# Row blocks turned by VectorE and exchanged by way of memory in place of TensorE transposes, for the middle sequences

## The chip, the cores and the metric

One core of one Trainium2 chip runs the whole program. The metric is the device time of one execution in microseconds, as the median of several runs. All data are 32-bit floats, apart from a few small 16-bit tables of the router.

## What is computed

The reference is one transformer layer on 8 sequences of 512 tokens with 256 features: causal attention with 16 heads of 128 (four heads share one key and value group), and a feed-forward part with a router that sends each token to 6 of 64 experts, beside one shared expert. Both parts normalize the rows ahead of their products and normalize what they add.

```python
x = x + _layernorm(attn(_layernorm(x), wq, bq, wkv, bkv, wo))
x = x + _layernorm(ffn(_layernorm(x), gate_w, w_gate, w_up, w_down, sh_gate, sh_up, sh_down))
# attn: q, k, v = x@wq + bq, x@wkv + bkv; q, k += sinusoids; softmax(causal(q k^T / sqrt(128))) v; @ wo
# ffn: top 6 of softmax(x@gate_w.T), each expert silu(x@w_gate) * (x@w_up) @ w_down, plus the shared expert
```

The kernel's matmuls take their operands with the dimension that is summed over on the partitions. A normalized block of rows has tokens on the partitions, so it must be turned, features onto partitions, before the projections (tile `xnt`, first half of the layer) and before the shared expert and the router (tile `xt2`, second half).

## The kernel before

A sequence is held as four tiles of 128 tokens. The main loop runs over 128 heads, k = 16 b + s for sequence b and head s. The order on each engine is written out by hand; every engine takes its instructions in that order. One round of the loop holds, in this order on TensorE:

- the scores of head k (`psc`, L289): four matmuls of 128, 256, 384 and 512 columns, for the causal shape. VectorE subtracts the mask and finds the least value (`e`, L293), ScalarE takes the exponential (L296). The scores go to the pool `ps_s` of three PSUM banks.
- the output projection of head k-3 (`po`, L361), the queries of head k+1 (`pq`, L276; VectorE adds bias and sinusoids to make `qt`, L279), and the weighting of the values of head k-2 (`pav`, L349).

Between these stand, on the other engines, `weigh(k)` on GpSimd (L306: `e` times the reciprocal of its sum) and `turned(k-1)`. The latter turns the weights of the head before: VectorE transposes blocks of 32 x 32 (`eb`, L322), SP writes the four groups of 32 partitions to memory (`ex_d`, L327), and SP reads the whole back (`et`, L330), so that blocks land on the partitions on which they belong. SP's queue waits for the four writes to land before it issues the read. `et` is wanted by `pav` one round later.

Beside the heads of a sequence b run two slower strands, tied to a head number and a place in the round (A, B, M, D, from the weigh to the end of the round):

- `prepare(b+1)`, the first half for the next sequence: load the rows of `x`, statistics (`scales`), normalize (`normal`, tile `xn`), `turn`, four `keys`, four `values`. Its steps are taken from an iterator `ahead`, so many in each round. For most sequences the rows are loaded at the end of head 6, normalized in head 8 ahead of the queries, and turned at the end of head 8.
- `feed_forward(b-1)`, the second half of the sequence before: `copies` 2D, `residual_sums` 4A, `store` 5B (SP writes `x1`, L774), `rows` 6A (tile `xg`), `turn` 6M, `shared_gate` 7A (`psg`, `psu`, L708, which read `xt2`), the router (`gate` at 8A, and the steps "r" after it), the other products of the shared expert (the steps "f").

Both call `transpose_rows`, in which TensorE turns 128 x 128 blocks into a PSUM bank of `ps_s`, and ScalarE copies one bank (L109), VectorE the other (L112) back. The tiles named here share tags with others: one buffer under "xn" holds `o`, then `xn`; one under "y" holds the router's logits `lg`, later `y`.

From head 94 on the experts' products run beside the heads (`routed`); sequences from EARLY = 5 on have a second half with more steps. These parts, and the end of the program, are as they were in the changed kernel.

Of the kernel before, what the change touches and what calls it, by code (L numbers as in the profile page):

```python
# [11 lines left out]
F32 = mybir.dt.float32  # L12
# [7 lines left out]
P = 128  # L20
B, T, E = 8, 512, 256
NT = B * T
NI = T // P
BS = 32
AT = [0, 4, 7, 9]
NB = AT[-1] + 1
NC = E // P
# [12 lines left out]
EARLY = 5  # L40
# [4 lines left out]
def sandwich_kernel(ctx, tc, x, wq, bq_t, wkv, bk_t, bv, wo, gate_wt, w_gate, w_up, w_down,  # L45
                    sh_gate_t, sh_up_t, sh_down_t, pe_t, out):
    nc = tc.nc
# [11 lines left out]


    ex_d = [dram.tile([P, NI, NB * BS], F32, tag=f"ex{n}_d", name=f"ex{n}_d") for n in range(2)]
    x1_d = dram.tile([NT, E], F32, tag="x1_d", name="x1_d")
    xg_d = dram.tile([ET_ROWS + 1, ROW], F32, tag="xg_d", name="xg_d")
    y_d = dram.tile([2 * (ET_ROWS + CAP), E], F32, tag="y_d", name="y_d")
# [49 lines left out]
    def transpose_rows(dst, rows, name):  # L114

        for c in range(NC):
            pt = ps_s.tile([P, T], F32, tag="s", name=f"pt_{name}_{c}")
            for i in range(NI):
                nc.tensor.transpose(pt[:, ts(i, P)], rows[:, i, ts(c, P)], ident)
            (on_act, on_dve)[c](dst[:, c, :], pt)  # L120


    with ExitStack() as part:
# [4 lines left out]
        p1 = pool("p1", 1)  # L128
# [96 lines left out]
        def prepare(b):  # L225

            s = seqs[b] = {"kt": []}

            def rows():
                s["x"] = load_x(b) if b else x_first  # L230

            def scales():
                s["scales"] = norm_scales(tiles_of(s["x"]), f"a{b}")

            def normal():
                mv, rs = s.pop("scales")
                s["xn"] = p1.tile([P, NI, E], F32, tag="xn", name=f"xn_{b}")
                for i in range(NI):
                    normalize(s["xn"][:, i, :], s["x"][:, i, :], mv, rs, i)

            def turn():
                s["xnt"] = p2.tile([P, NC, T], F32, tag="xnt", name=f"xnt_{b}")
                transpose_rows(s["xnt"], s["xn"], f"a{b}")

            def keys(g):
                pk = ps_m.tile([P, T], F32, tag="m", name=f"pk_{b}_{g}")
                for c in range(NC):
                    nc.tensor.matmul(pk, lhsT=wkv_sb[:, c, g, 0, :], rhs=s["xnt"][:, c, :],  # L248
                                     start=c == 0, stop=c == NC - 1)
# [12 lines left out]

            yield rows
            yield scales
            yield normal
            yield turn
            for g in range(G):
# [44 lines left out]
        def turned(k):  # L312
            l = live[k]
            eb = p2.tile([P, NI, NB, BS], F32, tag="eb", name=f"eb_{k}", bufs=1)
            for i in range(NI):
                for js in ([0, 1], [2, 3]):
                    js = [j for j in js if j <= i]
                    if not js:
                        continue
                    at, step = AT[js[0]] + i - js[0], AT[js[-1]] - AT[js[0]] - 1  # L320
                    blocks = eb[:, :, at : at + step * (len(js) - 1) + 1 : max(step, 1), :]
                    nc.vector.transpose(  # L322
                        blocks.rearrange("p c j t -> p j c t"),
                        l["e"][i][:, js[0] * P : (js[-1] + 1) * P].rearrange("p (j c t) -> p j c t", c=NI, t=BS))
            ex = ex_d[k % 2]
            for a in range(NI):
                nc.sync.dma_start(out=ex[:, a, :].rearrange("(c s) f -> s c f", s=BS),  # L327
                                  in_=eb[ts(a, BS)].rearrange("s c n t -> s c (n t)"))
            l["et"] = p2.tile([P, NI, NB, BS], F32, tag="et", name=f"et_{k}")
            nc.sync.dma_start(out=l["et"].rearrange("s a n t -> s (a n t)"), in_=ex.rearrange("p a f -> p (a f)"))  # L330

# [346 lines left out]
        def shared(b, xt2, l, banks="mmmmmm"):  # L678
# [22 lines left out]
            for n, (f0, fw) in reversed(list(enumerate(SH_CHUNKS))):  # L701
                mw = min(P, fw + NX // 2)
                pgu = []
                for w_sb, name in ((sg_sb, "psg"), (su_sb, "psu")):
                    tag = next(banks)
                    pp = {"m": ps_m, "s": ps_s}[tag].tile([P, T], F32, tag=tag, name=f"{name}_{b}_{n}")
                    for c in range(NC):
                        nc.tensor.matmul(pp[:mw, :], lhsT=w_sb[:, c, ds(f0, mw)], rhs=xt2[:, c, :],  # L708
                                         start=c == 0, stop=c == NC - 1)
                    pgu.append(pp)  # L710
                if fw < P:
# [40 lines left out]
        def feed_forward(b):  # L752
# [3 lines left out]
            l = {}  # L756
# [37 lines left out]
            def go(which, n=1):  # L794
                return lambda: [next(l[which]) for _ in range(n)]
# [7 lines left out]
            if b < B - 2:  # L803
                steps |= {"9A": go("f"), "9B": go("f"), "11A": go("f"), "11B": go("f")}
            if b < EARLY:
                return steps | {"10A": go("r"), "10D": go("r", 2),
                                "11D": go("r", 2), "12A": go("f"), "12D": go("r", 2), "13A": go("f"), "13D": go("r", 2)}
# [135 lines left out]
        def side(s, place):  # L943
            behind.pop(f"{s}{place}", lambda: None)()
            if not b:
                for u in rest.get(f"{s}{place}", ()):
                    u()

        for k in range(NK):
# [28 lines left out]
            if active and not finishing:  # L978
# [19 lines left out]
            for _ in range((0, 0, 0, 0, 0, 0, 1, 0, 1, 1, 2, 1, 1, 1, 2, 1)[s] if b == EARLY + 1 else  # L998
                           (0, 0, 0, 0, 0, 0, 1, 1, 1, 1, 1, 1, 1, 1, 2, 1)[s]):
                next(ahead, lambda: None)()  # L1000
# [97 lines left out]
```

## Time and profile before

| | |
|---|---|
| median of 3 runs | 1431.23 us (1428.58 to 1433.54) |
| profiled execution | 1433.63 us |
| its span, first to last instruction | 1431.9 us |
| mean granted TensorE clock | 0.995 |
| busy: TensorE, VectorE, ScalarE, GpSimd | 97%, 62%, 35%, 30% |
| DMA | 252.03 MB, mean 176 GB/s |
| HBM read, written | 143.01 MB, 107.74 MB |

The profile gives, for one execution, the busy time of each engine, the chain of work that ended last, groups of equal instructions with their mean duration and what ended the idle time before them, and on request windows and timelines. PE is TensorE, PEld its weight load, DVE VectorE, ACT ScalarE, POOL GpSimd, and SPq the queue of SP. L119 is line 119 of the kernel before. A 32-bit matmul is two instructions in the trace, a transpose one. Matmuls overlap, so a mean duration (0.593 us for a query's 512 columns) is longer than the distance from one to the next.

### The profile page before, as it was taken

The page shows a single profiled execution, that of the slowest core. Times are in us where ns is not written, and L with a number is a line of the kernel's source. Part 1 is how long each engine was busy: PE and PEld are TensorE (multiplying, and loading weights), DVE is VectorE, ACT ScalarE, POOL GpSimd, SP SyncE. Part 2 cuts the span into 40 slices and gives each one's busy share as a digit, 9 for nine tenths or more (in the row PEclk, how much of TensorE's full clock was granted, in tenths as well). Part 3 has the DMA queues.
Part 4 walks back from the last instruction along what each step waited for, and adds up shares of the span by engine and source line. Part 5 has one row for each costly group of instructions (what it writes and reads, how often), then busy time and mean ns, then how long its engine had stood idle before and what let it go on. Part 6 is the DMA issues. An engine that isn't in the chain of part 4 may idle for free.

```text
span 1431.9 us, 18567 instructions
## 1 busy us (share of the span) xinstructions
PE 1393.9 (97%) x5310; PEld 850.3 (59%) x5310; DVE 888.9 (62%) x3097; ACT 505.3 (35%) x1442; POOL 428.9 (30%) x686
## 2 busy tenths in 40 slices
PE   9999999999999999999999999999999999999895
PEld 5666665666656665656556665655556555556563
DVE  5565576656765576656765577566666545577634
ACT  2333333234422343234422343233443333444421
POOL 2231242113311232123211232124544344444311
PEclk9999999999999999999999999999999999999998
DMA  7765565356554564356544564358998789778702
GB/s 239 206 199 142 146 174 162 110 132 171 168 144 124 147 185 136 99 156 168 161 127 128 162 195 129 99 155 275 308 286 250 227 232 264 201 235 265 234 15 82
DMA packets 160791, 252.03 MB, mean 176 GB/s; under 512 B 16412, under 2 KB 136189, under 8 KB 160685
## 3 DMA queue, kind: packets, MB, share of 16 engines
q1 hardware_dynamic: 125869, 201.52, 48.4%
q10 hardware_dynamic: 28672, 39.85, 9.0%
q0 software_dynamic: 6144, 9.44, 3.3%
q8 instruction: 43, 0.70, 0.2%
q14 instruction: 63, 0.52, 0.1%
HBM read 143.01 MB, written 107.74 MB: 175 GB/s over the span
## 4 chain that ended last, share of the span: by engine, by line
PE 83%; DVE 8%; DMA 2%; ACT 2%; issue 2%; POOL 1%; SPq 0%; DVEq 0%; ACTq 0%; POOLq 0%
PE pav L349 17%; PE psc L289 16%; PE po L361 13%; PE pq L276 13%; PE pk L248 4%; PE pv L259 4%; PE psg L708 3%; PE psu L708 3%; PE pgu L549 2%; PE py L735 2%; DVE eb L322 2%; PE pd L575 2%; ACT e L296 2%; DMA ex_d<-eb 1%; PE pth L566 1%
## 5 line engine op out<-in xcount | busy, mean ns | idle before, releaser
L306 POOL TENSOR_SCALAR e<-e,recip 128x128 f32<-128x128 f32 x508 | 269.7, 571 | 775.3 <-DVE recip L303 762.4
L296 ACT ACTIVATE e<-e,least 128x128 f32<-128x128 f32 (+3 forms) x512 | 285.7, 559 | 350.4 <-DVE least L293 332.6
L289 PE MATMUL psc<-kt,qt 128*128 128x128 f32 (+3 forms) x1024 | 307.7, 438 | 9.9 <-DVE least L293 3.5
L349 PE MATMUL pav<-et,v 128*128 128x512 f32 (+3 forms) x1024 | 297.1, 433 | 1.4 <-DMA et<-ex_d 1.1
L349 PEld LDWEIGHTS pav<-et,v 128*128 128x128 f32 x1024 | 193.6, 190 | 161.0 <-issue 113.8
L293 DVE CUSTOM_DVE_ANT_0 e<-psc,mask 128x128 f32<-128x128 f32 (+3 forms) x512 | 232.2, 479 | 58.1 <-PE psc L289 52.2
L361 PE MATMUL po<-wo_sb,ao 128*128 128x256 f32 x1024 | 245.0, 383 | 0.7 <-ACT ao L109 0.7
L276 PE MATMUL pq<-xnt,wq_sb 128*128 128x512 f32 x512 | 240.9, 593 | 0.3 <-ACT sc L388 0.3
L361 PEld LDWEIGHTS po<-wo_sb,ao 128*128 128x128 f32 x1024 | 194.2, 191 | 72.5 <-issue 40.3
L109 ACT COPY ao<-pav 128x512 f32<-128x512 f32 x128 | 75.0, 586 | 435.8 <-PE pav L349 407.3
L322 DVE STREAM_TRANSPOSE eb<-e 128x128 f32<-128x128 f32 x756 | 227.5, 365 | 0.8 <-DMA ex_d<-eb 0.4
L289 PEld LDWEIGHTS psc<-kt,qt 128*128 128x128 f32 x1024 | 165.4, 190 | 85.3 <-DVE least L293 23.5
L279 DVE SCALAR_TENSOR_TENSOR qt<-pq,bq_sb,pe_sb 128x512 f32<-128x512 f32 x128 | 95.7, 748 | 106.0 <-PE pq L276 104.9
L276 PEld LDWEIGHTS pq<-xnt,wq_sb 128*128 128x128 f32 x512 | 95.9, 190 | 69.9 <-issue 64.0
L303 DVE RECIPROCAL recip<-total 128x4 f32<-128x4 f32 x128 | 22.8, 178 | 119.8 <-ACT e L296 119.8
L296 ACT ACTIVATION_READ_ACCUMULATOR e<-e,least 128x1 f32 x512 | 95.6, 187 | 0.0
L586 POOL DMA_INDIRECT y_d<-dd,idx x32 | 51.0, 1592 | 94.3 <-DMA y_d<-dd,idx 33.2
L248 PE MATMUL pk<-xnt,wkv_sb 128*128 128x512 f32 x128 | 60.3, 594 | 0.2 <-ACT xnt L109 0.2
L261 DVE TENSOR_TENSOR v<-pv,bv_sb 128x512 f32<-128x512 f32 x32 | 22.1, 691 | 60.8 <-PE pv L259 60.8
L259 PE MATMUL pv<-wkv_sb,xnt 128*128 128x512 f32 x128 | 59.1, 593 | 0.0
L251 DVE SCALAR_TENSOR_TENSOR kt<-pk,bk_sb,pe_sb 128x512 f32<-128x512 f32 x32 | 24.0, 750 | 47.5 <-PE pk L248 47.5
L112 DVE COPY ht<-pth 88x256 f32<-88x256 f32 x32 | 13.4, 418 | 55.2 <-PE pth L566 52.5
(197 smaller groups left out, 1113.6 us busy)
## 6 DMA issues: line engine op xcount, KB each, us to landing
ex_d<-eb SPq DMA_DIRECT2D x504, 160.0 KB
et<-ex_d SPq DMA_DIRECT2D x126, 640.0 KB
wgu<-in_w_gate ACTq DMA_DIRECT2D x32, 352.0 KB
wgu<-in_w_up ACTq DMA_DIRECT2D x32, 352.0 KB
wd<-in_w_down ACTq DMA_DIRECT2D x32, 352.0 KB
y<-y_d ACTq DMA_DIRECT2D x10, 512.0 KB
x<-in_x SPq DMA_DIRECT2D x8, 512.0 KB
x_d<-x SPq DMA_DIRECT2D x8, 512.0 KB
```

The source lines that it names most:

```text
L248: nc.tensor.matmul(pk, lhsT=wkv_sb[:, c, g, 0, :], rhs=s["xnt"][:, c, :], start=c == 0, stop=c == NC - 1)
L259: nc.tensor.matmul(pv, lhsT=s["xnt"][:, c, ts(i, P)], rhs=wkv_sb[:, c, :, 1, :], start=c == 0, stop=c == NC - 1)
L276: nc.tensor.matmul(pq, lhsT=wq_sb[h // QPG][:, c, ts(h % QPG, D)], rhs=seqs[b]["xnt"][:, c, :], start=c == 0, stop=c == NC - 1)
L279: nc.vector.scalar_tensor_tensor(qt, pq, bq_sb[:, h : h + 1], pe_sb, ALU.add, ALU.add)
L289: nc.tensor.matmul(psc[:, :w], lhsT=l["qt"][:, ts(i, P)], rhs=seqs[b]["kt"][h // QPG][:, :w], start=True, stop=True)
L293: nc.vector.tensor_tensor_reduce(out=e, in0=psc[:, :w], in1=mask[:, T - w :], scale=-1.0 / math.sqrt(D), scalar=BIG, op0=ALU.add, op1=ALU. ...
L296: nc.scalar.activation(e, e, AF.Exp, bias=l["least"][:, i : i + 1], scale=-1.0, accum_out=l["total"][:, i : i + 1])
L306: engine.tensor_scalar(e, e, recip[:, n : n + 1], 1.0, ALU.mult, ALU.mult)
L322: nc.vector.transpose(blocks.rearrange("p c j t -> p j c t"), l["e"][i][:, js[0] * P : (js[-1] + 1) * P].rearrange("p (j c t) -> p j c t", ...
L349: nc.tensor.matmul(pav[:, :, j:, :], lhsT=seqs[b]["v"][:, j, ts(g, D)], rhs=l["et"][:, :, AT[j] : AT[j] + NI - j, :], start=j == 0, stop=j ...
L361: nc.tensor.matmul(po[b][i // 2][:, i % 2, :], lhsT=ao[:, ts(i, P)], rhs=wo_sb[:, h, :], start=h == 0 and i % 2 == 0, stop=h == NH - 1, sk ...
L708: nc.tensor.matmul(pp[:mw, :], lhsT=w_sb[:, c, ds(f0, mw)], rhs=xt2[:, c, :], start=c == 0, stop=c == NC - 1)
```

## The change

The first half of sequences 1 to 6 and the second half of sequences 0 to 3 no longer use `transpose_rows`. In `exchange_rows`, VectorE turns the 32 x 32 blocks of the four row tiles (four instructions of 128 x 256), SP writes the blocks by groups of 32 partitions to memory (`exr_d`, four DMAs of 128 KB), and a read of the whole (512 KB) is put on a list, `readings`. The next `turned` issues that read on SP between its own four writes and its own read.

What lands has its tokens in another order, (a, c, i, t) with token 128 i + 32 a + t and feature half c. For the second half the gate products read it through a permuted access (`in_order`, `as_taken`). For the first half GpSimd sorts it into `xnt` with two copies of 128 x 512 (a new step, `sort`).

The steps of these parts move. In sequences 0 to 5, `prepare` now loads in head 6 ahead of the queries, normalizes in head 8 behind the queries, turns in head 9 ahead of the queries, sorts at the end of head 10, and makes keys and values in heads 11 to 15. For the second half of sequences 0 to 3 every step after head 6 comes one head later.

```diff
+    exr_d = [dram.tile([P, NI, NC * NI * BS], F32, tag=f"exr{n}_d", name=f"exr{n}_d") for n in range(2)]
...
+    def exchange_rows(dst, rows, blocks, ex):
+        for i in range(NI):
+            nc.vector.transpose(blocks[:, :, :, i, :].rearrange("p k c t -> p c k t"),
+                                rows[:, i, :E].rearrange("p (c k t) -> p c k t", c=NC, t=BS))
+        for a in range(NI):
+            nc.sync.dma_start(out=ex[:, a, :].rearrange("(k s) f -> s k f", s=BS),
+                              in_=blocks[ts(a, BS)].rearrange("s k c i t -> s k (c i t)"))
+        readings.append(lambda: nc.sync.dma_start(out=dst().rearrange("p a c i t -> p (a c i t)"),
+                                                  in_=ex.rearrange("p a f -> p (a f)")))
...
             def turn():
+                if 0 < b <= EARLY + 1:
+                    blocks = p1.tile([P, NI, NC, NI, BS], F32, tag="y", name=f"xb_a{b}")
+                    def rows():
+                        s["rows"] = p1.tile([P, NI, NC, NI, BS], F32, tag="y", name=f"xr_a{b}")
+                        return s["rows"]
+                    exchange_rows(rows, s["xn"], blocks, exr_d[0])
+                    return
...
+            def sort():
+                s["xnt"] = p2.tile([P, NC, T], F32, tag="xnt", name=f"xnt_{b}")
+                for c in range(NC):
+                    nc.gpsimd.tensor_copy(as_taken(s["xnt"][:, c, :], s["rows"]), in_order(s["rows"], c))
...
@@ turned, between the writes of ex and the read of et @@
+            while readings:
+                readings.pop()()
...
-                        nc.tensor.matmul(pp[:mw, :], lhsT=w_sb[:, c, ds(f0, mw)], rhs=xt2[:, c, :],
+                        nc.tensor.matmul(as_taken(pp[:mw, :], xt2), lhsT=w_sb[:, c, ds(f0, mw)], rhs=in_order(xt2, c),
...
@@ feed_forward @@
             def turn():
+                if b < EARLY - 1:
+                    l["xt2"] = p1.tile([P, NI, NC, NI, BS], F32, tag="xt2", name=f"xt2_{b}")
+                    blocks = p1.tile([P, NI, NC, NI, BS], F32, tag="xn", name=f"xb_f{b}")
+                    exchange_rows(lambda: l["xt2"], l["xg"], blocks, exr_d[1])
+                    return
...
+                return steps if b == EARLY - 1 else {
+                    f"{int(at[:-1]) + (int(at[:-1]) > 6)}{at[-1]}": step for at, step in steps.items()}
...
-            if s == (9 if b == EARLY + 1 else 8):
-                next(ahead, lambda: None)()
+            if s == 9 and b <= EARLY + 1:
+                next(ahead)()
+            if s == 6 and b <= EARLY:
+                ahead = prepare(b + 1)
+                next(ahead)()
             if k + 1 < NK:
                 queries(k + 1)
...
             side(s, "M")
+            if b <= EARLY and s == 8:
+                next(ahead)()
...
-            if s == 6 and b + 1 < B:
+            if s == 6 and b == EARLY + 1:
                 ahead = prepare(b + 1)
...
-                           (0, 0, 0, 0, 0, 0, 1, 1, 1, 1, 1, 1, 1, 1, 2, 1)[s]):
+                           (0, 0, 0, 0, 0, 0, 0, 1, 0, 0, 1, 1, 2, 1, 2, 2)[s]):
```

More of the change, by code (lines that the diff above doesn't have):

```diff
@@ L120, in transpose_rows, with in_order, as_taken @@
             (on_act, on_dve)[c](dst[:, c, :], pt)
+    readings = []
+    def exchange_rows(dst, rows, blocks, ex):
[7 more added lines that the diff above has]
+                                                  in_=ex.rearrange("p a f -> p (a f)")))
+    def in_order(xt, c):
+        return xt[:, c, :] if len(xt.shape) == 3 else xt[:, :, c, :, :].rearrange("p a i t -> p i a t")
+    def as_taken(out, xt):
+        return out if len(xt.shape) == 3 else out.rearrange("p (i a t) -> p i a t", i=NI, a=NI)
     with ExitStack() as part:
@@ L266, in prepare @@
             yield turn
+            if 0 < b <= EARLY + 1:
+                yield sort
             for g in range(G):
@@ L805, in feed_forward @@
             if b < EARLY:
[L806 to L807 removed]
+                steps |= {"10A": go("r"), "10D": go("r", 2),
+                          "11D": go("r", 2), "12A": go("f"), "12D": go("r", 2), "13A": go("f"), "13D": go("r", 2)}
+                return steps if b == EARLY - 1 else {
+                    f"{int(at[:-1]) + (int(at[:-1]) > 6)}{at[-1]}": step for at, step in steps.items()}
             def mark():
@@ L994, in sandwich_kernel @@
             side(s, "D")
-            if s == 6 and b + 1 < B:
+            if s == 6 and b == EARLY + 1:
                 ahead = prepare(b + 1)
-            for _ in range((0, 0, 0, 0, 0, 0, 1, 0, 1, 1, 2, 1, 1, 1, 2, 1)[s] if b == EARLY + 1 else
-                           (0, 0, 0, 0, 0, 0, 1, 1, 1, 1, 1, 1, 1, 1, 2, 1)[s]):
-                next(ahead, lambda: None)()
+            for _ in range((0, 0, 0, 0, 0, 0, 1, 0, 1, 1, 2, 1, 1, 1, 2, 1)[s] if b == EARLY + 1 else 0 if b > EARLY else
+                           (0, 0, 0, 0, 0, 0, 0, 1, 0, 0, 1, 1, 2, 1, 2, 2)[s]):
+                next(ahead)()
             twice = active and k > EARLY * NH + NH
```

## The prediction

> **What bounds the kernel now.** I read the page's busy times and its chain first: TensorE is busy 97% of the span at full clock and makes up 83% of the chain. Time can be won only where TensorE is emptied or stops waiting.
>
> ```profile
> PE 1393.9 (97%) x5310; PEld 850.3 (59%) x5310; DVE 888.9 (62%) x3097; ACT 505.3 (35%) x1442; POOL 428.9 (30%) x686
> ...
> PE 83%; DVE 8%; DMA 2%; ACT 2%; issue 2%; POOL 1%; SPq 0%; DVEq 0%; ACTq 0%; POOLq 0%
> ```
>
> Next the groups with shapes kept apart, for the operations removed and the rows nearest to those added:
>
> ```profile
> L119 PE MATMUL pt_f<-ident,xg 128*128 128x128 f32 x64 | 12.7, 292 | 2.9 <-DVE xg L106 2.5
> ...
> L119 PE MATMUL pt_a<-ident,xn 128*128 128x128 f32 x64 | 8.3, 273 | 0.0
> ...
> L322 DVE STREAM_TRANSPOSE eb<-e 128x256 f32<-128x256 f32 x504 | 183.7, 403 | 0.0
> ...
> L112 DVE COPY xnt<-pt_a 128x512 f32<-128x512 f32 x8 | 5.4, 679 | 3.8 <-PE pt_a L119 3.8
> ...
> L306 POOL TENSOR_SCALAR e<-e,recip 128x512 f32<-128x512 f32 x127 | 93.4, 735 | 0.0
> ```
>
> Third, windows cut at the first score of a head. They show a plain head (head 4 of sequence 1), then heads 6, 7, 8 and 9, which hold both turns. Columns: length, then busy time of PE, PEld, DVE, ACT, POOL.
>
> ```profile
> 189.50:197.26 7.76, 7.76 (x30) 5.01 (x29) 6.58 (x26) 3.11 (x9) 3.48 (x6) 1.00 0.62 170
> ...
> 205.03:214.81 9.78, 9.30 (x38) 5.84 (x37) 7.28 (x27) 3.69 (x10) 3.24 (x5) 1.00 0.66 189
> 214.81:226.00 11.19, 11.19 (x38) 6.52 (x37) 7.01 (x22) 4.84 (x12) 2.06 (x4) 1.00 0.75 223
> 226.00:235.22 9.22, 9.22 (x42) 6.12 (x41) 8.08 (x32) 5.00 (x19) 3.19 (x5) 1.00 0.38 89
> 235.22:249.16 13.94, 13.45 (x42) 7.29 (x41) 8.30 (x34) 3.95 (x11) 2.06 (x4) 1.00 0.58 156
> ```
>
> A plain head is 7.76 us with TensorE always busy, so I take 7.76 as the floor, and 1.71 for two 512-column matmuls of a projection (head 7: 7.76 + 2 x 1.71 = 11.18, seen 11.19). Last, TensorE's timeline where sequence 1's rows are turned in the second half (head 6 of sequence 2) and where the head after the other turn starts:
>
> ```profile
> 367.34 1.88 PE L276 MATMUL pq<-xnt,wq_sb 128*128 128x512 f32 x4
> 369.06 0.67 PE L119 MATMUL pt_f<-ident,xg 128*128 128x128 f32 x2
> 369.88 0.33 PE L119 MATMUL pt_f<-ident,xg 128*128 128x128 f32 x1 [0.15 <-DVE xg L106]
> 370.47 0.77 PE L119 MATMUL pt_f<-ident,xg 128*128 128x128 f32 x5 [0.27 <-DVE xg L106]
> 371.07 2.32 PE L349 MATMUL pav<-et,v 128*128 128x512 f32 x8
> ...
> 395.23 1.77 PE L289 MATMUL psc<-kt,qt 128*128 128x384 f32 x4 [0.38 <-DVE xnt L112]
> ```
>
> The eight pt_f cost 2.0 us (369.06 to 371.07) because they start before VectorE has normalized xg. The third score of head 9 waits for VectorE's copy of pt_a, which still holds a bank of ps_s.
>
> **What the Trainium skill says.** "TensorE: Matmul & The Clock Gate", Part 4, puts a transpose at about 275 ns in a kernel, with a copy out of PSUM after it; the trace agrees (273 ns). But pipelined, eight take 1.04 us. "VectorE: DVE Perf Modes", The three transpose paths, says VectorE turns 32x32 blocks only, into SBUF; hence the trip through memory. "DMA: Bandwidth & Descriptors", Issuing engines are not separate DMA queues, says all DMAs share 16 engines: the new ones queue with ex and et. The trace agrees: in head 6 of sequence 1 the ex writes queued behind the x1 store land about 4.5 us after their issue, not the usual 2.8 (semaphore updates in the trace). The same page, Two DMAs through the same engine are not ordered, says the issuer must wait for a write to land before reading it. SP does so here: last ex write issued by 368.4, et read issued at 371.24.
>
> **The change, part by part.** Ten turns leave TensorE: the first half of sequences 1 to 6 and the second half of 0 to 3. That is 80 transposes, ten ScalarE copies (0.59 each) and ten VectorE copies (0.68). In come 40 block transposes, 40 writes and 10 reads on SP, and 12 GpSimd copies.
>
> *Second half, four times.* Head 6 falls from 9.78 to 7.76: **-2.02 each, -8.1**. VectorE's four transposes: six eb transposes (ten 128-blocks) take 1.81 in the timeline, so four of two blocks take 8/10 of that, 1.45 (by the mean, at most 4 x 0.403 = 1.61). They follow qt, which ends at head +7.62, so they reach 1.3 us into head 7. Behind them on VectorE stand e of the first score, normally at 0.43, and then everything of that head. The fourth score needs the bank which that e frees and is due at 1.28; e is done at about 1.5. I take **+0.2 each, +0.8** (0 to 0.5). Later work of head 7 fits: its gate products have moved to head 8.
>
> *First half, sequences 2 to 5 (prepared beside the second half of 0 to 3), four times.* Head 8 is 9.22, where 7.76 plus the pg transposes and their wait (8.32) would do: -0.90. Head 9 is 13.94 against 7.76 + 3 x 1.71 = 12.90: -1.04. **-1.94 each, -7.8.** In its place xn goes behind qt in head 8, which is 11.19 long now and covers it. In head 9 VectorE does recip (to 5.2), most, the transposes (to 6.85), qt (to 7.6; the scores need it at 8.3), then the router's chain, 1.96, to about 9.5. That is 1.2 into head 10, and e is again just late: **+0.1 each, +0.4** (0 to 0.8).
>
> *Sequence 1* (no second half beside it): heads 8 and 9 take 8.63 and 9.87 instead of 7.76 and 9.47: **-1.3**. *Sequence 6*: the second half beside it is not moved a head, so xn (2.0) and the router's chain (2.0) both stand behind qt in head 8. The first e of head 9 starts at about 2.7 and holds the fourth score 1.7 us: 1.94 - 1.7, **-0.2**.
>
> *GpSimd*: two copies per first-half turn, 0.74 each by the nearest row, up to double for the permuted read: 1.5 to 3 us. They wait for the read, which I put at about 10 us into head 10, and the keys want them at 7.8 into head 11: hidden. Queued behind them is weigh, due at 5.3 in head 11: reached in time.
>
> *Permuted xt2 in the gate products*: runs of 32 elements. The 128-column form of pav reads such runs at the time of the contiguous form of psc (274 against 276 ns): nothing, both ways.
>
> *SP and the 16 engines, first half*: four more issues of 0.46 and a read. Issued after et, the writes are ahead of the next ex, which VectorE does not finish before 3.0. The read waits for writes a head old. Only sequence 0, where SP still sends the zeros and et lands with 0.3 to 0.6 us to spare, may pay: **+0.5** once (0 to 1.5).
>
> *Second half's return, the doubtful part.* SP's timeline in sequence 2:
>
> ```profile
> 363.36 0.43 SPq L774 DMA_DIRECT2D x_d<-x  x1
> 366.50 1.87 SPq L327 DMA_DIRECT2D ex_d<-eb  x4
> 371.24 0.34 SPq L330 DMA_DIRECT2D et<-ex_d  x1
> 371.68 0.40 SPq L144 DMA_DIRECT2D x<-in_x  x1
> ```
>
> New head 7 starts at 371.2. The new writes are issued at 372.5 but queue behind this et and x, whose packets end at 375.8. The x1 store, also 512 packets of 1 KB, took 1.55: packets to 377.3, landing 0.45 later, 377.8. SP waits for that, then issues the read; the head's ex packets go ahead of it to about 379.0; the read takes 1.5 (et, 640 KB, takes 1.9) and lands 0.8 later, at 381.3 to 381.8. Head 8 starts at 379.1 and wants xt2 at +2.2, 381.3. I take **+0.4** for three sequences, and **+1.4** in the first, where et goes out 1.1 later: **+2.6** in all. Bounds: 0, and 2.5 each if packets interleave less well. Queued behind the wait on TensorE is everything; behind SP's wait stands et, due a head later with over 3 us to spare.
>
> Sum: -8.1 - 7.8 - 1.3 - 0.2 = -17.4; +0.8 + 0.4 + 0.5 + 2.6 = +4.3; **-13**. The profiled execution took 1433.63 (span 1431.9), giving 1420.6; the median shown lies 2.4 lower, giving **1418 us**, 0.9% less. About 0.3% (4.3 us) is what a measurement of this kernel can tell from no change.
>
> **Rivals.** *The late return eats most.* xt2 comes 2.5 us late in all four: 17.4 - 1.7 - 10 = 5.7, hence 1425.5; at 3 us, 1427.5. For it: et took 3.5 to 4.8 us to land here, and the chain of four transfers has no slack. Against: the queue empties in every head. *Slower, by the same wait*: without it the sum is -15.7, so at 3.9 us each the gain is gone and from 5 us it is a loss of over 0.3%; at 5.5, 1437. It needs ex and the read to take twice what the trace shows. *Nothing comes of it*: VectorE, 62% busy on average but 8.1 of 9.2 us in head 8, becomes the bound of heads 7, 9 and 10, and the scores wait 1.5 us in each of these: 4 x 4.5 = 18 cancels the gain, 1431. Against: the fourth score's margin of 0.85 us above. That the transposes are not removed can be left out: the changed program's order on TensorE lacks all 80 and adds no matmul.
>
> **How the numbers follow.** Forecast 0.68 (1412 to 1425); late return 0.17, two thirds of it still faster by over 0.3%; slower 0.09; nothing 0.06. Faster 0.68 + 0.11 = 0.79, same 0.06 + 0.06 = 0.12, slower 0.09. If all small costs are nothing, the time is 1414; I reach 2 below for waits that I don't see, and up to 1429 for the late return.
>
> **What would show it.** Right: head 6 at 7.8, heads 8 plus 9 of sequences 1 to 4 without pt_a, DVE's busy time up by about 9 (40 x 0.36 less 10 x 0.68 is 8), gate products idle on xt2 by 0 to 1.5. Wrong: gate products waiting over 2 us for DMA in each sequence, scores waiting for e by over 1 us in heads 7, 9 or 10, or pav waiting for et.

## The result, and the profile after

The changed kernel takes 1429.74 us (median; 1424.18 to 1434.22) beside 1433.19 us for the kernel before on the same chip: a ratio of 0.9967, 95% interval 0.9956 to 0.9977. It is faster by 0.33%, 3.5 us, where 13 were forecast. The profiled spans, 1427.6 and 1431.9 us, differ by 4.3. I split them at the first score of head 96, ahead of the experts' products:

| span, us | before | after | difference | forecast |
|---|---|---|---|---|
| ahead of sequence 0's first score | 18.31 | 17.91 | -0.4 | 0 |
| sequence 0 | 140.16 | 141.93 | +1.8 | -0.8 |
| sequences 1 to 4 | 633.93 | 624.75 | -9.2 | -12.1 |
| sequence 5 | 158.87 | 158.00 | -0.9 | -0.2 |
| from head 96 on | 480.6 | 485.0 | +4.4 | 0 |

Of the 13 us forecast, 4.4 are missing by head 96 (5.5 in sequences 0 to 4, less 1.1 in the other rows), and 4.4 more after it, in instructions that the change doesn't touch.

The page's busy times and its chain, after:

```profile
PE 1383.4 (97%) x5230; PEld 841.4 (59%) x5230; DVE 895.4 (63%) x3127; ACT 500.2 (35%) x1432; POOL 433.7 (30%) x698
...
PE 80%; DMA 7%; DVE 7%; issue 2%; ACT 2%; POOL 1%; SPq 1%; ACTq 0%; DVEq 0%; POOLq 0%
```

TensorE lost its 80 transposes and 10.5 us of busy time, and the span got only 4.3 of them. In the chain the share of DMA rose from 2% to 7%. The groups of the added operations (busy time and mean ns of one, then the idle time ahead of them):

```profile
L130 DVE STREAM_TRANSPOSE xb_f<-xg 128x256 f32<-128x256 f32 x16 | 5.6, 405 | 0.0
L280 POOL COPY xnt<-xr_a 128x512 f32<-128x512 f32 x12 | 7.0, 611 | 17.1 <-DMA xr_a<-exr_d 17.1
L749 PE MATMUL psg<-xt,sg_sb 128*128 128x512 f32 x84 | 39.8, 596 | 4.7 <-DMA xt<-exr_d 4.7
```

The permuted products cost what contiguous ones do (the row above holds both; the median is 592 ns up to 720 us, where all are permuted, and 592 ns after it), and the sort is cheap. Heads 6 to 10 of sequence 1 by windows (length, then busy PE, PEld, DVE, ACT, POOL):

```profile
206.41:214.17 7.76, 7.76 (x31) 5.01 (x29) 6.72 (x27) 3.10 (x9) 3.23 (x5) 1.00 0.79 239
214.17:222.16 7.99, 7.99 (x31) 4.93 (x29) 6.64 (x24) 3.00 (x9) 2.05 (x4) 1.00 0.85 263
222.16:235.05 12.89, 11.43 (x38) 6.44 (x37) 7.56 (x28) 4.86 (x12) 3.07 (x5) 1.00 0.69 214
235.05:243.40 8.35, 8.35 (x34) 5.25 (x33) 6.83 (x27) 4.38 (x17) 2.05 (x4) 1.00 0.37 84
243.40:254.66 11.26, 11.26 (x38) 6.44 (x37) 7.71 (x33) 3.48 (x10) 3.06 (x6) 1.00 0.85 239
```

Head 6 is the plain head forecast. Head 7 is 0.23 longer than one, head 10 0.07 over its 11.19. Head 8, which now holds the gate products, is 1.7 over its 11.19 here, and TensorE is idle for 1.46 of it. TensorE's waits (us in total, times, longest), and its timeline in head 11 of sequence 0, then in head 8 of sequence 2:

```profile
PE psc L328 <- DVE least L332: 6.0, 6, 2.4
PE psg L749 <- DMA xt<-exr_d: 4.7, 4, 1.5
PE pav L390 <- DMA et<-ex_d: 3.0, 3, 2.3
PE pd L616 <- DMA wd<-in_w_down: 2.9, 2, 2.1
PE ptx L579 <- DMA gx<-xg_d,idx: 2.3, 1, 2.3
```
```profile
112.76 2.42 PE L390 MATMUL pav<-et,v 128*128 128x512 f32 x8 [2.29 <-DMA et<-ex_d]
...
381.84 1.96 PE L749 MATMUL psg<-xt,sg_sb 128*128 128x512 f32 x4 [0.89 <-DMA xt<-exr_d]
```

Four of these five waits are for a DMA. For the first of these (psg) the forecast had 2.6 us, and for the next (pav) up to 1.5. For the two of the experts (pd, ptx) it had no change; the kernel before waits 1.9 us at ptx and has no wait at pd in its list.

### The profile page after: what moved, and what is told of

Read it like the earlier page. It is cut to its first block, busy times and chain, and to the rows that moved or that the text cites. A ratio compares the mean times of both kernels' runs of the same rounds, so it can differ in the third digit from the quotient of the medians.

```text
span 1427.6 us, 18526 instructions
## 1 busy us (share of the span) xinstructions
PE 1383.4 (97%) x5230; PEld 841.4 (59%) x5230; DVE 895.4 (63%) x3127; ACT 500.2 (35%) x1432; POOL 433.7 (30%) x698
## 4 chain that ended last, share of the span: by engine, by line
PE 80%; DMA 7%; DVE 7%; issue 2%; ACT 2%; POOL 1%; SPq 1%; ACTq 0%; DVEq 0%; POOLq 0%
PE pav L390 16%; PE psc L328 15%; PE pq L315 13%; PE po L402 13%; PE pk L285 4%; PE pv L296 4%; PE psg L749 3%; PE psu L749 3%; PE pgu L590 2%; PE py L776 2%; PE pd L616 2%; DMA wd<-in_w_down 2%; DVE eb L361 1%; DMA exr_d<-xb_f 1%; ACT e L335 1%
```

## The experiments

Every ratio is to the kernel before on the same chip, whose median was 1432.7 to 1434.9 us. The medians of gate_behind, gate_zero, gate_zero_last and gate_zero_fill rest on 6 executions each, that of fill on 7. The stretches come from one trace each. "Wait" in the last column is TensorE's ahead of the first transpose of gathered rows (`gx`, head 98); it ended with the gather in all kernels but moved_late, where VectorE came last.

| kernel | median, us; ratio [95%] | seq 0 | seq 1-4, mean | head 96 at | head 96 to end | wait |
|---|---|---|---|---|---|---|
| before | | 140.2 | 158.5 | 951.3 | 480.6 | 1.89 |
| before_again | 1432.5 (one run) | 140.9 | 158.5 | 951.3 | 479.5 | 1.69 |
| after | 1429.74; 0.9967 [0.9956, 0.9977] | 141.9 | 156.2 | 942.6 | 485.0 | 2.27 |
| after_again | 1428.5 (one run) | 140.9 | 156.4 | 942.3 | 484.4 | 1.90 |
| first_only | 1433.61; 0.9996 [0.9984, 1.0009] | 141.3 | 157.7 | 947.3 | 484.5 | 3.06 |
| second_only | 1435.42; 1.0007 [0.9996, 1.0017] | 140.4 | 159.0 | 952.8 | 480.3 | 2.60 |
| moved_late | 1429.57; 0.9976 [0.9965, 0.9987] | 139.8 | 157.2 | 946.2 | 481.9 | 1.52 |
| pool_queue | 1433.66; 0.9991 [0.9975, 1.0006] | 141.1 | 157.3 | 945.8 | 488.2 | 2.02 |
| gate_behind | 1424.80; 0.9942 [0.9920, 0.9964] | 143.5 | 155.5 | 942.0 | 483.3 | 3.10 |
| gate_zero | 1422.57; 0.9920 [0.9897, 0.9943] | 138.9 | 155.5 | 936.9 | 486.5 | 2.28 |
| exr_last | 1429.51; 0.9974 [0.9959, 0.9989] | 141.0 | 156.3 | 942.4 | 483.0 | 2.45 |
| gate_zero_last | 1423.38; 0.9923 [0.9903, 0.9944] | 138.9 | 155.5 | 936.2 | 489.1 | 2.87 |
| before_room | 1434.29; 1.0009 [0.9996, 1.0023] | 140.2 | 158.5 | 951.1 | 480.9 | 1.70 |
| six_back | 1428.66; 0.9969 [0.9954, 0.9984] | 141.8 | 156.5 | 944.2 | 482.8 | under 0.7 |
| six_only | 1433.28; 1.0004 [0.9990, 1.0019] | 140.2 | 158.5 | 950.4 | 484.2 | 2.35 |
| gate_zero_six_back | 1425.84; 0.9942 [0.9922, 0.9962] | 139.6 | 155.3 | 937.9 | 489.8 | under 0.7 |
| fill | 1425.25; 0.9934 [0.9909, 0.9958] | 142.7 | 156.1 | 943.5 | 480.0 | 0.28 |
| gate_zero_fill | 1419.38; 0.9890 [0.9864, 0.9916] | 139.0 | 155.5 | 936.4 | 482.2 | under 0.7 |

before_again and after_again are the two kernels unchanged, for the scatter between traces of one kernel: sequence 0 differs by 0.7 to 1.0 us, the stretch from head 96 by 0.5 to 1.1.

> The kernel before once more, for a second trace: head 96 at 951 within 1; after it 480.6 within 1 if the 4 us that the kernels with a moved first half lose there are caused by them, 480 to 486 if it is chance.

> The changed kernel once more, for a second trace. The span is split at the first score of head 96, ahead of the experts' products: 951.3 + 480.6 us in the kernel before, 942.6 + 485.0 in the changed one. Up to head 96 everything follows hand-written order with little spread: 942.6 within 0.7. After head 96: if the 4.4 us lost there are chance (arrival of the experts' weights differing from one execution to the next), anything from 479 to 487; if the change causes them, 485 within 1.

### The two halves alone

```diff
@@ first_only: second halves turned by TensorE, not moved a head @@
-                if b < EARLY - 1:
+                if b < 0:
...
-                return steps if b == EARLY - 1 else {
+                return steps if b < EARLY else {
@@ second_only: first halves turned by TensorE, load and steps at their old places @@
-                if 0 < b <= EARLY + 1:
+                if b < 0:
...
-            if s == 6 and b <= EARLY:
-                ahead = prepare(b + 1)
-                next(ahead)()
...
-            if s == 6 and b == EARLY + 1:
+            if s == 6 and b + 1 < B:
```

> Only the first half (sequences 1 to 6) goes through memory; the second half of sequences 0 to 3 stays on TensorE and is not moved a head. If the gains and losses add up turn by turn as in the changed kernel's trace: sequence 0 loses 1.8 (et late in head 11), sequences 1 to 5 gain 0.9 each as sequence 5 does there, so head 96 starts about 3 us earlier than in the kernel before (948.5). If VectorE's load is what counts (normalizing and the router's chain both behind the queries' qt in head 8), the fourth score of head 9 waits 1 us or more in each sequence. After head 96: 479 to 487 by chance; 485 if the new tiles in memory or the first half's order cause the loss; 480.6 if the second half does.

> Only the second half of sequences 0 to 3 goes through memory, moved a head as in the changed kernel; the first half stays on TensorE at its old place. Head 6 gains 2.0, head 7 loses 0.2, the gate products of head 8 wait for xt2 by 1.0 to 1.7, and head 9 loses the 1.0 us wait for the copy of pt_a because the router's chain is gone from head 8: about -1.5 per sequence, four times, head 96 at 945. No loss in sequence 0. If instead the late xt2 were caused by the first half's extra transfers, the gate products would not wait here and head 96 came at 940. After head 96: as for the first.

first_only gains 0.8 us a sequence, second_only loses 0.5, both together gain 2.3: the parts don't add up. In first_only head 9 of sequence 1 still starts its gate products 1.0 late, without any transpose near it. TensorE's line there, and VectorE's last lines ahead of it:

```profile
236.68 1.12 PE L328 MATMUL psc<-kt,qt 128*128 128x512 f32 x2 [0.79 <-DVE least L332]
```
```profile
236.20 0.23 DVE L439 MAX8 top<-xg 128x8 f32<-128x64 f32 x1
236.35 0.27 DVE L332 CUSTOM_DVE_ANT_0 e<-psc,mask 128x128 f32<-128x128 f32 x1
```

The head starts at 234.42, but `e` runs only at 236.35, behind the router's chain of MAX8. That chain is late here because `xn` (1.40 us) has moved to a place ahead of it. In the kernel before (head 9 starts at 235.22) the copy of `pt_a` stood in the same queue:

```profile
235.94 0.23 DVE L398 MAX8 top<-xg 128x8 f32<-128x64 f32 x1
236.08 0.67 DVE L112 COPY xnt<-pt_a 128x512 f32<-128x512 f32 x1
236.67 0.28 DVE L293 CUSTOM_DVE_ANT_0 e<-psc,mask 128x128 f32<-128x128 f32 x1
```

So the 1.04 us that I gave to `pt_a` and its bank came from the chain and the copy together. In second_only, where the copy stays and the chain is gone from this place, head 9 loses about 0.4 us: its gate transposes (`pg`) start 2.65 us into it, against 2.26 in moved_late, which has no copy there.

second_only leaves the load of `x` at the end of head 6, so on SP it comes behind the four new writes. SP's queue in head 7 (start 212.21), VectorE in head 8 (start 220.21), and TensorE in head 8:

```profile
213.43 1.83 SPq L133 DMA_DIRECT2D exr_d<-xb_f  x4
215.30 0.78 SPq L167 DMA_DIRECT2D x<-in_x  x1
```
```profile
221.63 1.41 DVE L78 BATCH_NORM_STATS2 st_a<-x 128x6 f32<-128x256 f32 x4 [2.62 <-DMA x<-in_x]
```
```profile
223.77 1.93 PE L328 MATMUL psc<-kt,qt 128*128 128x512 f32 x2 [2.10 <-DVE least L332]
225.50 2.82 PE L749 MATMUL psg<-xt,sg_sb 128*128 128x512 f32 x4
```

`x` lands 1.4 us into head 8 (its landing in the trace). VectorE, in order, stands 2.62 us at the statistics of `x`, with `e` behind them, and TensorE waits 2.10 for a bank. That head takes 16.1 us. In the changed kernel the load is issued ahead of the four writes, and VectorE does not wait for it there; so the move of the load is no detail, though no run has it alone. Of the 2.82 us of psg, more below.

### The order without the exchange

moved_late has the changed kernel's order of steps, but TensorE's transposes: the first half at head 9 ahead of the queries, the second half in head 7 behind the scores.

```diff
-                if 0 < b <= EARLY + 1:
+                if b < 0:
...
-                if b < EARLY - 1:
+                if b < 0:
...
+                moved["7A"] = moved.pop("6M")
```

> The changed kernel's order of steps without its exchange: all turns on TensorE with copies by ScalarE and VectorE, the second half's turn put in head 7 behind the scores, when xg is long normalized, so that it costs its 1.04 us alone. If most of the changed kernel's gain is the order (no wait for xg, no pt_a bank held while VectorE runs the router's chain), sequences 1 to 4 take about 157.0 us each against 158.4 before and 156.3 in the changed one, sequence 0 139.9, and head 96 comes at about 944.5, within 2 us of the changed kernel. If emptying TensorE is what pays, sequences 1 to 4 stay at 158 or above.

Head 96 comes 5.1 us earlier than before, of 8.7 in the changed kernel. Of what the change brings ahead of head 96, over half is order. A sequence gains about 1.3 us, and most of it is the 1.04 of head 9, whose gate products no longer stand behind the router's chain and the copy. The second half's turn brings almost nothing: it still costs 1.88 us in head 7, against 2.02 in head 6 before, because the transposes now wait 0.76 us for a bank that VectorE frees late. Had they cost their 1.04 us alone, as expected, this version would have gained 0.8 us more a sequence (an estimate). Its median is that of the changed kernel.

### The late return

gate_behind puts the output projection ahead of the gate products in head 8 of sequences 1 to 4, which gives `xt2` 1.7 us more.

```diff
+                gates, products = moved.pop("8A"), moved.pop("8B")
+                moved["8B"] = lambda: (gates(), products())
```

> The changed kernel with one swap on TensorE in head 8 of sequences 1 to 4: the output projection (1.7 us) comes ahead of the gate products, so these want xt2 at 3.9 us into the head and not at 2.2. If the late return of xt2 is what the forecast mis-sized, its waits (1.6, 1.0, 1.5 and 1.3 us beyond 2.2) go: head 8 falls from 12.3 to 12.9 to about 11.2, head 96 comes 5 to 5.5 us earlier (937.3), and the kernel is about 0.3 to 0.4% faster than the changed one. If VectorE or the products' banks are the bound there, head 8 keeps its length. After head 96: 485 if systematic, 479 to 487 by chance.

The wait for `xt2` is gone from the list of TensorE's waits, and sequences 1 to 4 take 155.5 instead of 156.2: 2.9 us in all. Head 8 falls to 11.75 to 12.09 us, not to 11.2: of the 5.7 us lost there half comes back. The swap has a price of its own: 11.75 is also what head 8 takes in every sequence of gate_zero_six_back, 0.56 over 11.19, and the list of waits shows 0.3 of it in each of the four heads, in pav, which now waits for the gate's `gs`. Head 96 is not earlier in this trace because head 11 of sequence 0 took 14.1 in it, with a half clock behind its wait of 2.70. The ratio, 0.9942 beside the changed kernel's 0.9967, points to a gain, but their intervals just overlap.

pool_queue issues the second half's four writes and its read on GpSimd's queue instead of SP's.

```diff
-                    exchange_rows(lambda: l["xt2"], l["xg"], blocks, exr_d[1])
+                    exchange_rows(lambda: l["xt2"], l["xg"], blocks, exr_d[1], nc.gpsimd)
```

> The changed kernel with the second half's five DMAs issued by GpSimd and not by SP, so that they don't stand behind et and the load of x in SP's ring. If it is the place in that ring that makes xt2 late, it lands up to 2 us earlier and head 8 falls to about 11.2 in sequences 1 to 4, et and x a little later. If the 16 engines' throughput is what counts, head 8 stays at 12.3 to 13.5. GpSimd may be held by the read's wait, so that weigh in head 7 is late; then eb and the scores of head 8 wait.

GpSimd's timeline there (head 8 starts at 220.90):

```profile
214.41 2.52 POOL L133 DMA_DIRECT2D exr_d<-xb_f  x4 [1.75 <-DVE least L332]
222.97 0.58 POOL L135 DMA_DIRECT2D xt<-exr_d  x1 [6.04 <-DMA exr_d<-xb_f]
```

In this sequence, the first, the writes on GpSimd's queue land 5.7 to 6.2 us after their issue (4.7 to 5.5 on SP's in the changed kernel), and `weigh` stands behind GpSimd's wait of 6.04. Head 8 takes 16.6 us here, part of it at half clock. In the other three sequences the writes land 3.7 to 4.8 us after their issue (4.4 to 5.5 on SP's), but they are issued later in the head, and the read lands 11.2 to 11.8 us into head 7, against 11.1 to 11.5. Head 8 stays at 12.4 to 13.1 us (12.3 to 12.7). So leaving SP's queue does not bring `xt2` back sooner. That all queues run on the same 16 engines is what "DMA: Bandwidth & Descriptors" of the Trainium skill (Issuing engines are not separate DMA queues) says; this run agrees, though it does not separate the engines from the later issue.

### Sequence 0

gate_zero is gate_behind with SP's zero stores held back in heads 7 to 11 of sequence 0; they follow in heads 12 to 15.

```diff
-            if not b:
+            if not b and not 7 <= s < 12:
```

> The kernel with the output projection ahead of the gate products (gate_behind), and the stores of zeros held back in heads 7 to 11 of sequence 0 and made later. If the late et of head 11 there comes from the backlog of zeros and the row exchange on SP's queue, head 11 falls from 11.5 to 14.1 us to about 9.5, sequence 0 from 141 to 143.5 to about 139, and head 96 comes at about 938. If the exchange alone overfills the queue in heads as short as 7.76 us, a wait of 1 us or more stays in head 11.

SP's timeline of the changed kernel (head 11 starts at 104.70), then of gate_zero (104.29):

```profile
106.33 0.34 SPq L371 DMA_DIRECT2D et<-ex_d  x1
106.72 0.92 SPq L236 DMA_DIRECT2D y_d<-zero  x2
108.20 2.44 SPq L366 DMA_DIRECT2D ex_d<-eb  x4
115.05 0.34 SPq L371 DMA_DIRECT2D et<-ex_d  x1
```
```profile
104.38 0.34 SPq L371 DMA_DIRECT2D et<-ex_d  x1
107.33 2.02 SPq L366 DMA_DIRECT2D ex_d<-eb  x4
111.61 0.34 SPq L371 DMA_DIRECT2D et<-ex_d  x1
```

`et` goes out 1.62 us into head 11 in the changed kernel, 0.09 in gate_zero. Head 11 falls from 12.03 to 9.53 us and sequence 0 to 138.9, which is the forecast gain of 1.3 without any backlog.

### After head 96

Instructions there are the same in every kernel without the fill. Three theories were tried. The place of the new buffers in memory, with exr_d laid out last (exr_last, gate_zero_last), and with two buffers put into the kernel before that nothing reads (before_room):

```diff
@@ exr_last, and gate_zero_last in the same way on gate_zero @@
-    exr_d = [dram.tile([P, NI, NC * NI * BS], F32, tag=f"exr{n}_d", name=f"exr{n}_d") for n in range(2)]
...
     ly_d = dram.tile([NT - ET_ROWS, E], F32, tag="ly_d", name="ly_d")
+    exr_d = [dram.tile([P, NI, NC * NI * BS], F32, tag=f"exr{n}_d", name=f"exr{n}_d") for n in range(2)]
@@ before_room, on the kernel before @@
+    exr_d = [dram.tile([P, NI, 256], F32, tag=f"exr{n}_d", name=f"exr{n}_d") for n in range(2)]
...
+    for d in exr_d:
+        nc.gpsimd.dma_start(out=d[:, 0, :NI], in_=mhalf)
```

> The changed kernel with the two new buffers in memory (exr_d) laid out behind all the others instead of ahead of x1_d, xg_d and y_d; nothing else differs. Question: the stretch after the first score of head 96, whose instructions are the same in every kernel, takes 483.3 to 488.2 us in six traces of kernels whose first half goes through memory and 479.5 to 481.9 in four without. Theory 'addresses' (x1_d, xg_d and y_d lie 1 MB further on, and the experts' gathers and weights then share memory less well): the stretch takes 480 us here, head 96 stays at 942.5, median about 1425. Theory 'the exchange leaves something behind' (rings, order of the queues): the stretch takes 484 to 486, median about 1430. I put 0.4 on addresses.

> The kernel with the output projection ahead of the gate products in head 8 and the zero stores held back in heads 7 to 11 of sequence 0 (gate_zero), with exr_d behind all other buffers in memory. With addresses as the cause, head 96 stays at 936.9 and the stretch after it falls from 486.5 to about 480, median about 1417; with the exchange as the cause, 1423 as before.

> The kernel before with two buffers of 512 KB in memory at exr_d's place, into each of which GpSimd's queue writes one 2 KB tile at the start and which nothing reads; no exchange. With addresses as the cause, head 96 stays at 951.3 and the stretch after it rises from 480 to about 485, median about 1437; with the exchange as the cause, 480 and no change, 1432.5.

All three say no: 483.0, 489.1 and 480.9. Then the last exchange, that of sequence 6, which ends just ahead of the stretch (six_back takes it out, gate_zero_six_back does so on gate_zero, six_only has it alone):

```diff
@@ six_back; sequence 5 also takes the steps of the kernel before @@
-                if 0 < b <= EARLY + 1:
+                if 0 < b <= EARLY:
@@ six_only; sequences 0 to 4 also take the steps of the kernel before @@
-                if 0 < b <= EARLY + 1:
+                if b == EARLY + 1:
```

> The changed kernel with sequence 6's first half as before (its rows turned by TensorE in head 8 of sequence 5, keys and values at their old places); the exchanges of sequences 1 to 5 and of the four second halves stay. Sequence 5 then takes 158.87 us as before, 0.87 more. Theory 'the last exchange': what stands ahead of head 96 in sequence 5 costs the 3 to 5 us after head 96; then the stretch after head 96 takes 480 to 481.5 us and the median is about 1426. Theory 'any first half by way of memory' leaves something behind: the stretch takes 483 to 486, median about 1430.5.

> The kernel before with sequence 6's first half alone by way of memory, its steps at their new places; everything else as before. Theory 'the last exchange': sequence 5 takes 158.0, the stretch after head 96 rises from 480 to 483 to 486 us, median 1435 to 1437. Theory 'any first half by way of memory' with more than one exchange needed, or chance: the stretch takes 480 to 481, median 1432.

> The best version so far (the output projection ahead of the gate products in head 8, zero stores held back in heads 7 to 11 of sequence 0) with sequence 6's first half as before. Head 96 at 936.5 + 0.9 = 937.5. If the last exchange is what costs time after head 96, that stretch falls from 486 to 489 us to about 481, median about 1419; if not, 1424.

It explains one place and not the sum. With it, the wait for `gx` in head 98 is 1.90 to 3.10 us in all nine traces without the fill; without it, at most 1.89 in six of seven. But where it was taken out, other waits grew (head 100, heads 103 to 105), and the stretch stays at 482.8 and 489.8.

The third is the clock. Windows of the changed kernel from its ptx on, with the granted clock behind the busy times:

```profile
965.60:969.00 3.40, 3.40 (x5) 1.33 (x4) 0.87 (x3) 0.00 (x0) 2.29 (x3) 0.50 1.02 364
969.00:972.53 3.53, 3.53 (x19) 1.97 (x17) 0.93 (x6) 1.51 (x4) 0.00 (x0) 1.00 0.51 150
1051.00:1054.30 3.30, 1.20 (x10) 0.69 (x11) 2.83 (x11) 0.96 (x3) 0.08 (x1) 1.00 1.04 213
1054.30:1057.70 3.40, 3.40 (x15) 1.62 (x12) 0.49 (x2) 2.81 (x13) 0.00 (x0) 0.50 0.96 304
```

Behind the wait of 2.27 us for `gx`, and behind that of 2.10 for `wd`, TensorE is granted half its clock for 3.4 us: 1.7 us lost on top of each wait. The kernel before waited 1.89 in head 98 and kept its clock; exr_last waited 2.45, longer than the changed kernel, and kept it too (two lines of each):

```profile
973.18 0.48 PE L538 MATMUL ptx<-ident,gx 128*128 128x128 f32 x2 [1.89 <-DMA gx<-xg_d,idx]
973.50 1.88 PE L276 MATMUL pq<-xnt,wq_sb 128*128 128x512 f32 x4
...
964.87 0.48 PE L579 MATMUL ptx<-ident,gx 128*128 128x128 f32 x2 [2.45 <-DMA gx<-xg_d,idx]
965.18 1.88 PE L315 MATMUL pq<-xnt,wq_sb 128*128 128x512 f32 x4
```

The traces of all kernels give the price. Less its wait, head 98 takes 10.0 us in each of the seven traces that wait 1.5 us or more and keep the clock, and 11.4 to 11.7 in the seven that lose it. fill puts eight matmuls of the identity ahead of the first ptx, which touches no transfer:

```diff
+            for n in range(8 if key == 0 else 0):
+                nc.tensor.matmul(pt[:, 0, :], lhsT=ident, rhs=ident, start=True, stop=True)
             for c in range(2):
                 nc.tensor.transpose(pt[:, c, :], rows[:, c, :], ident)
```

> The changed kernel with eight matmuls of the identity by itself (128 columns, about 0.21 us each by the 0.85 us of 512 columns) put ahead of the first turn of gathered rows (ptx, head 98), where TensorE waits 1.9 to 3.1 us for the gather; the transposes then write over what they leave. Question: in the traces a wait of 1.9 us or more is followed in most cases by 3.4 us in which half the clock is granted. Theory 'the clock': filling most of the wait keeps the clock whole, head 98 takes about 12.3 us instead of 13.6 to 14.0, the gather's own lateness of 0.4 us stays; the stretch after head 96 falls by 1.7 us, to 483 or less, median 1428.5. Theory 'it is the late gather alone': head 98 stays at 13.6 to 14.0 with half clock or with the landing later by as much, median 1429.7.

> The best version so far (the output projection ahead of the gate products in head 8, zero stores held back in heads 7 to 11 of sequence 0) with the same eight matmuls ahead of the first ptx. By the clock: head 98 at about 12.3 instead of 13.8, no half clock in it, median about 1421.5 instead of 1422.6. Otherwise no change.

TensorE's timeline in head 98, of the changed kernel and then of fill:

```profile
964.88 0.48 PE L579 MATMUL ptx<-ident,gx 128*128 128x128 f32 x2 [2.27 <-DMA gx<-xg_d,idx]
965.19 3.25 PE L315 MATMUL pq<-xnt,wq_sb 128*128 128x512 f32 x4
```
```profile
963.37 1.95 PE L579 MATMUL ptx<-ident 128*128 128x128 f32 x16
965.59 0.51 PE L581 MATMUL ptx<-ident,gx 128*128 128x128 f32 x2 [0.28 <-DMA gx<-xg_d,idx]
965.94 1.88 PE L315 MATMUL pq<-xnt,wq_sb 128*128 128x512 f32 x4
```

The gather arrives as late as before (ptx at 6.1 us into head 98, against 6.3), but the queries behind it take 1.88 us instead of 3.25, and head 98 takes 12.10 instead of 13.97. gate_zero_fill keeps its clock in head 98 as well. Since three of ten long waits without the fill kept it too, two traces are good evidence for the fill and no proof. The stretch falls to 480.0, more than the one head gives: heads 103 to 105 (53.1 instead of 55.4, with no half clock this time) and 119 to 125 (67.6 instead of 70.5) are shorter in this trace too. For these later heads the trace shows that, but no run shows why. The medians agree with a gain (ratio 0.9934 beside 0.9967, 0.9890 beside 0.9920), but in each pair the intervals overlap. gate_zero_fill, 1419.38 us or 1.1% below the kernel before, is the fastest version that I ran.

## Why the prediction was wrong

Three terms of the sum failed: the return of `xt2` (3.1 us too small), the late `et` of sequence 0 (2.6 too small), and the rest of the program, put at nothing and worth 4.4.

**What held.** Head 6 fell to 7.76. Four block transposes took 1.41 us (1.45 forecast), head 7 came out at 7.99 (7.96), head 10 0.07 over (0.1). The sort took 0.61 us a copy, less than the lower bound, and stayed hidden. The permuted products cost nothing. VectorE did not become the bound.

**The return of `xt2`, +2.6 forecast, 5.7 measured** (head 8 over 11.19: 1.71, 1.13, 1.52, 1.35). The mechanism was right, the size was not. SP's queue in head 7 of sequence 2, which starts at 370.63:

```profile
370.84 0.34 SPq L371 DMA_DIRECT2D et<-ex_d  x1
371.28 0.40 SPq L167 DMA_DIRECT2D x<-in_x  x1
371.85 2.19 SPq L133 DMA_DIRECT2D exr_d<-xb_f  x4
374.10 3.01 SPq L366 DMA_DIRECT2D ex_d<-eb  x4
378.10 0.34 SPq L135 DMA_DIRECT2D xt<-exr_d  x1
```

In this head the four writes landed at 6.38 to 7.45 us by the landings in the trace; by the forecast the last was due at 6.6. The read went out at 7.46, behind the ex writes, and landed at 11.1, 3.1 us into head 8, where the forecast had 10.1 to 10.6. The failing step is the end of the packets of `x`, behind which the writes queue. I put it at 4.6 us into the head (375.8) and the landing of `x` at 5.05. In the kernel before about nine tenths of its packets had ended by then, but the last of them ended at 376.36, and SP waits for the last: `x` landed at 376.77, 5.1 us after its issue. In the changed kernel it was issued 0.2 later in the head and landed 5.4 us after that, 6.0 into the head. Behind it the last of the writes took 1.4 us more (1.55 forecast) and the read 3.6 (3.5 to 4.0), so those terms held. That leaves 0.3 us for the transfers in flight together; the DMA engines are busy for 85% of head 7 in the window shown. Without the wait a sequence takes 155.3 (gate_zero_six_back), 0.9 less than in the changed kernel, though the swapped projection costs 0.56 of its own there.

**Sequence 0, +0.5 forecast (bound 1.5), +3.1 measured** (-1.3 + 3.1 = +1.8; in the second trace about 1 less). 2.5 of it are in head 11, which gate_zero brings back to 9.5 us, and 0.5 in head 8, which the second trace does not have. I had seen that SP still sends zeros there and took one late landing. I left out that writes, zeros, ex and the read also delay the issue of the next `et`, by 1.5 us, and then its landing, 6.4 us after the issue.

**Sequence 5, -0.2 forecast, -0.9 measured.** I had `e` start 2.7 us into head 9, behind 2.0 of xn and 2.0 of the router, and hold the fourth score for 1.7 us. But xn took 1.40 us; `e` started at 1.9 and held the score for 1.0, as long as before the change. The first half's -1.04 in the other sequences was put down to the copy of `pt_a` alone. There the sum came out by luck: the gain came because the gate products moved away from the router's chain as well; in sequence 5, where they did not, the wait of 1.0 stayed.

**The rest of the program, 0 forecast, +4.4 measured.** This is the step that I never examined. Head 98 gives +2.1 (0.4 of wait and a half clock of 1.7), heads 103 to 105 +3.7 (a half clock, and about 2 of waits for weights), heads 106 to 126 +0.5; the last part of the program is 1.8 shorter, where both kernels wait 2.20 us and only the kernel before has a half clock behind it. So the changed kernel has two half clocks there and the kernel before one: the clock's part of the 4.4 is about 1.7, and what is left is waiting. That the gather and the weights land some tenths later is only observed: all eleven traces of kernels with a first half through memory and no fill have 482.8 us or more from head 96 on, the five without 481.9 or less. That the exchange itself does this is not shown. moved_late, which has the new order and no exchange, lost no clock there and took 481.9; the changed kernel's two traces, less 1.7 us for each half clock (an estimate), come to 481.6 and 482.7, and those of the kernel before to 478.9 and 479.5. The new order alone may thus bring much of it. The cause of what is left beside the clock stays open.

**The rivals.** "The late return eats most" was the nearer story, at 1.4 us a sequence in place of 2.5, and the rest of the loss stood in no rival.

## What to carry to other kernels

Price a DMA chain by the landing of its last packet, measured with the same neighbours in flight, not by the time at which most packets have ended; and give every consumer of it a reserve, as one swapped step (the projection ahead of the gate products) brought 2.9 us. Before calling the rest of a program untouched, look for waits of about 2 us there: where 0.4 us more of waiting came with a half clock, it cost 2.1. Try the new order of steps with the old operations first; here it gave over half of the gain by itself.

## What the runs showed of the hardware

- TensorE's clock falls to half for 3.4 us behind single waits of 1.9 to 3.1 us, though not behind each, and the length alone does not decide. Ahead of the first gather it did so in seven of ten waits of 1.9 us or more without the fill, and in none of the four of 1.5 to 1.89; the three that kept it were 2.45, 2.87 and 3.10 us long. One wait of 2.0 to 2.2 us near the end, which all 18 traces have, was followed by a half clock in seven. Shorter waits close together may do it as well: 1.15 and 1.81 us, starting 3.2 us apart, in gate_zero_last. "TensorE: Matmul & The Clock Gate" of the Trainium skill (HAM oscillation — how this bites in real kernels) warns of idle gaps over about 3.4 us; here gaps of 2 us were enough in many cases, and the measurement decides. In second_only, too, psg takes 2.82 us behind a wait of 2.10, and the trace shows half clock there:

```profile
224.00:227.40 3.40, 3.40 (x5) 1.34 (x5) 2.86 (x12) 1.86 (x7) 0.62 (x1) 0.50 0.76 238
```

- GpSimd copies 128 x 512 floats through a permuted read in 0.61 us, less than its scaling of a contiguous tile of that size (0.73).
- A queue of its own did not bring the exchange back sooner: with the same traffic around, the writes landed 5.7 to 6.2 us after their issue on GpSimd's queue in one sequence and 3.7 to 4.8 in three, on SP's 4.4 to 5.5, and the read landed no sooner in the head.
